# Attention probabilities turned by VectorE and DMA instead of TensorE in a fused Flamingo-style block

## The chip, the core and the metric

The kernel runs on one core of one Trainium2 chip. The core has five engines, each with its own queue of instructions that runs strictly in order: TensorE (PE, matrix products into PSUM), VectorE (DVE), ScalarE (ACT), GpSimd (POOL) and SyncE (SP, which here only issues DMA transfers). They meet through semaphores. The metric is the time of one execution on the device, in microseconds (us); less is better.

## The reference

Four steps follow each other for a batch of four sequences of 512 tokens with 512 features, all in float32:

```
x = x + tanh(g_x[0]) * ((1 - gamma) * layernorm(x) + gamma * A)          # A: sigmoid(sim), the best 30% of each row, made symmetric
x = x + tanh(g_f[0]) * bitlinear_ffn(layernorm(x))                       # Hadamard turns, 8-bit activations, ternary weights
x = x + tanh(g_x[1]) * latent_attention(layernorm(x), ctx)               # 16 heads, see below
x = x + tanh(g_f[1]) * bitlinear_glu(layernorm(x))
```

The change lies in the third step. For each head:

```
q_big  = rope(hidden @ Wq_h.T @ w_kc_q_h)      # 384 wide
kv_r   = rope(ctx)                             # 512 x 128 for a sequence, shared by all heads
scores = (q_big @ W_qr_h) @ (kv_r @ W_kr_h).T  # 64 wide product, 512 x 512 scores
attn   = softmax(scores)
ctx_c  = attn @ kv_r                           # 512 x 128
out   += ctx_c @ w_kc_kv_h.T @ Wo_h.T          # the two weights are multiplied once, ahead: "om", 128 x 512
```

## The kernel before, in words

A sequence is held as four token tiles of 128 tokens (one per partition) with 512 features. The work falls into a long prologue (first step of sequence 0, first feed-forward, weights), an attention phase from about 286 us to the end of the 32nd pair, and a tail (second feed-forward of the last sequence).

The attention phase is a generator, `attention`, that walks over 32 **pairs**: sequence `b` from 0 to 3 and in it `g` from 0 to 7, a pair being two heads of one sequence. For the pair at hand it goes over the four token tiles `j`, and mixes in the query work of the pair that comes next:

- `scores(j)` (lines 855 to 878) makes the 128 x 512 scores `pss` of both heads (two 64-row products that run side by side in the array), DVE finds the row maximum `nm` (L871), ACT takes the exponential `pp` (L874), DVE inverts the sum (L876) and ACT scales `pp` (L877).
- `head` (L804) and `rope` (L819 to L833) make the next pair's queries, products on PE, rotation on DVE and POOL (`ro`, `rs`).
- `turn(j)` turns the probabilities of a tile: four 128 x 128 products with the identity per head on PE (`ppt`, L885), copied from PSUM into `pT` by ACT (L886). It is called two tiles late (`turn(j - 2)`), and the last two calls come after the loop.
- after the loop `rotated` makes the next pair's `qr` (`pr`, L790 and L792, copied by ACT in L850); then `attended` multiplies all 512 turned rows by `kv` (`pc`, L893, copied to `cxo` by ACT in L898), and `added` multiplies by `om` and adds to the residual (`po`, L905, and DVE in L910).

A float32 product of 128 x 128 by 128 x 512 shows as two matmul records in the profile.

Beside the pairs runs background work in slices: while sequence `b` is in attention, the first step of `b + 1` (`adjacency`: a chain of MAX8 and MATCH_REPLACE8 on DVE, L486 and L491, which finds the threshold of the best 30%), its key projections (`keys`) and its feed-forward (`feed0`); during the last sequence the second feed-forward of the first three. A list of jobs with costs and due times sets how much background work each tile of a pair yields. The order on each engine is then fixed when the program is built, by a scheduler with priorities; the top-k chain carries a lowered priority and so fills the places that others leave on DVE.

All loads of weights (`wq`, `wc`, `wr`, `om`, `kr`) and the turns of quantized activations by DMA (L202) are issued from SP, in order. Every DMA of that queue uses one of eight completion semaphores in turn, and waits until the DMA that used it before has landed.

Of the kernel before, what the change touches and what calls it, by code (L numbers as in the profile page):

```python
# [9 lines left out]
F32 = mybir.dt.float32  # L10
# [5 lines left out]
P = 128  # L16
# [5 lines left out]
DC = 128  # L22
# [12 lines left out]
def flamingo_kernel(  # L35
# [51 lines left out]
    def front_t(name):  # L87
        if mine("front", 2):
            return two_k("front", 3, name)
        return wp.tile([P, 512], F32, tag="pp", name=name, bufs=7)  # L90

    def gate_t(name):
        if alone[0]:
# [597 lines left out]
    om_d, kr_d = {}, {}  # L691
    spilled = {}

    def ahead():

        cos_k = wp.tile([P, NT, DC], F32, tag="rs", name="cos_k", bufs=3)
        nc.gpsimd.dma_start(cos_k, cosk)
        sin_k = wp.tile([P, NT, DC], F32, tag="rs", name="sin_k", bufs=3)  # L700
        nc.gpsimd.dma_start(sin_k, sink)
        hf = DC // 2
        for b in range(B):
            cb = wp.tile([P, NT, DC], F32, tag="qh", name=f"cb_{b}")
            nc.gpsimd.dma_start(cb, cx[b * S : (b + 1) * S, :].rearrange("(j p) d -> p j d", p=P))
            t = const.tile([P, NT, DC], F32, tag=f"kv{b}", name=f"kv_{b}")
            nc.gpsimd.tensor_tensor(t, cb, cos_k, ALU.mult)
            rt = wp.tile([P, NT, DC], F32, tag="rs", name=f"rt_{b}", bufs=3)
            nc.gpsimd.tensor_tensor(rt[:, :, :hf], cb[:, :, hf:], sin_k[:, :, :hf], ALU.mult)
            nc.gpsimd.tensor_tensor(rt[:, :, hf:], cb[:, :, :hf], sin_k[:, :, hf:], ALU.mult)  # L710
            nc.gpsimd.tensor_tensor(t, t, rt, ALU.add)
            kv[b] = t
        yield
        for h in range(NH):
            wv = hp.tile([P, DC], F32, tag="wk", name=f"wv_{h}", bufs=3)
            nc.sync.dma_start(wv, wkckv[h])
            wo = wp.tile([P, D], F32, tag="rs", name=f"wo_{h}", bufs=3)
            nc.sync.dma_start(wo, woT[h])
            po = mm_ps(f"pO_{h}")
            nc.tensor.matmul(po, wv, wo, start=True, stop=True)  # L720
            om = wp.tile([P, D], F32, tag="cxo", name=f"oms_{h}", bufs=3)
            nc.scalar.copy(om, po)
            d = dram.tile([P, D], F32, tag=f"om{h}", name=f"omd_{h}")
            nc.gpsimd.dma_start(d, om)
            om_d[h] = d
            yield
        yield from keys(0)
# [25 lines left out]
    def hidden_T(b):  # L753
        mv, r = ln_stats([xs[b, j] for j in range(NT)], f"q{b}")
        t = hp.tile([P, NC, S], F32, tag="hT", name=f"hT_{b}", bufs=1)
        for j in range(NT):
            n = wp.tile([P, D], F32, tag="pp", name=f"nq_{b}_{j}", bufs=7)
            ln_tile(n, xs[b, j], j, mv, r)
            pt = tr_ps(f"phT_{b}_{j}")
            for c in range(NC):  # L760
                nc.tensor.transpose(pt[:, c, :], n[:, c * P : (c + 1) * P], ident)
            nc.scalar.copy(t[:, :, j * P : (j + 1) * P], pt)
        hT[b] = t
# [30 lines left out]
    class Pair:  # L794
# [41 lines left out]
        def rotated(self):  # L836

            wr, ros, u = self.wr, self.ros, self.u
            self.kr = wp.tile([P, S], F32, tag="kr", name=f"kr_{u}", bufs=1)
            nc.sync.dma_start(self.kr, kr_d[self.b, self.g])  # L840
            pr = mm_ps(f"pr_{u}")
            for o in range(3):
                at = 2 * o * 64
                halves(
                    pr, (wr[:, at : at + 64], wr[:, at + 64 : at + P]),
                    (ros[0, o], ros[1, o]) if o < 2 else (ros[2, 0], ros[2, 1]),
                    start=(o == 0), stop=(o == 2),
                )
            self.qr = wp.tile([P, S], F32, tag="qr", name=f"qr_{u}", bufs=1)
            nc.scalar.copy(self.qr, pr)  # L850
            self.pT = [
                wp.tile([P, NT, S], F32, tag="pT", name=f"pT_{u}_{i}") for i in range(2)
            ]

        def scores(self, j):

# [11 lines left out]
            for i in range(2):  # L868
                v = f"{self.u}_{i}_{j}"
                nm = small.tile([P, 1], F32, tag="nm", name=f"nm_{v}")  # L870
                nc.vector.tensor_reduce(nm, pss[i], AX.X, ALU.max, negate=True)  # L871
                pp = wp.tile([P, S], F32, tag="pp", name=f"pp_{v}", bufs=7)
                sm = small.tile([P, 1], F32, tag="sm", name=f"sm_{v}")
                nc.scalar.activation(pp, pss[i], AF.Exp, bias=nm, accum_out=sm)  # L874
                rs = small.tile([P, 1], F32, tag="rsm", name=f"rsm_{v}")
# [2 lines left out]
                self.pps[i, j] = pp  # L878

        def turn(self, j):  # L880
            for i in range(2):
                pt = tr_ps(f"ppt_{self.u}_{i}_{j}")
                pp = self.pps.pop((i, j))
                for l in range(NT):
                    nc.tensor.transpose(pt[:, l, :], pp[:, l * P : (l + 1) * P], ident)  # L885
                nc.scalar.copy(self.pT[i][:, :, j * P : (j + 1) * P], pt)  # L886

        def attended(self):
            self.cxo = []
            for i in range(2):  # L890
                pc = mm_ps(f"pc_{self.u}_{i}")
                for l in range(NT):
                    nc.tensor.matmul(  # L893
                        pc, kv[self.b][:, l, :], self.pT[i][:, l, :],
                        start=(l == 0), stop=(l == NT - 1),
                    )
                cxo = wp.tile([P, S], F32, tag="cxo", name=f"cxo_{self.u}_{i}", bufs=3)
                nc.scalar.copy(cxo, pc)  # L898
                self.cxo.append(cxo)

        def added(self):
            for j in range(NT):
                po = mm_ps(f"po_{self.u}_{j}")
                for i in range(2):
                    nc.tensor.matmul(  # L905
                        po, self.cxo[i][:, j * P : (j + 1) * P], self.oms[i],
                        start=(i == 0), stop=(i == 1),
                    )
                t = xs[self.b, j]
                nc.vector.scalar_tensor_tensor(t, po, tgx1, t, ALU.mult, ALU.add)  # L910
# [6 lines left out]
    def attention(first):  # L917


        order = [(b, g) for b in range(B) for g in range(NG)]  # L920
        cur = first
        for at, (b, g) in enumerate(order):
            nxt = begin(*order[at + 1]) if at + 1 < len(order) else None
            cur.oms = out_weights(b, g)
            fresh = nxt is not None and nxt.b != b
            for j in range(NT):
                cur.scores(j)
                if nxt:
# [8 lines left out]
                        nxt.rope(1)  # L937
                    else:
                        nxt.rope(2)
                if j > 1:  # L940
                    cur.turn(j - 2)
                yield b, g
            cur.turn(NT - 2)
            cur.turn(NT - 1)
            if nxt:
                nxt.rotated()
            cur.attended()
            cur.added()
            if g == NG - 1 and b < B - 1:
                for j in range(NT):  # L950
                    d = dram.tile([P, D], F32, tag=f"xd{b}_{j}", name=f"xd_{b}_{j}")
                    nc.sync.dma_start(d, xs[b, j])
                    spilled[b, j] = d
            cur = nxt

# [45 lines left out]
    def before(b):  # L1003
        k = keys(b)
        for n, cost in enumerate(adjacency(b)):
            yield cost
            if n % 6 == 5:

                with tc.high_priority(offset=-FILL // 4):
                    step(k, 1)  # L1010
# [168 lines left out]
```

## Time and profile before

| | |
|---|---|
| time, median of 3 runs | 2046.22 us (2045.72 to 2049.57) |
| profiled execution, span from first to last instruction | 2048.8 us |
| busy: PE, DVE, ACT, POOL | 1819.6, 1630.3, 1081.8, 336.1 us |
| mean granted TensorE clock | 0.960 |
| DMA moved | 151.90 MB, mean 74 GB/s |

The span of the profiled execution lies 2.6 us above the median of the runs, and inside their spread; nothing else of that execution's time is recorded. Busy times are sums over the span, so they are averages of stages that differ: the table of windows in the prediction shows the stages one by one. The page's groups name an instruction by line, engine and what it writes and reads, then its count, its busy time, the mean duration of one, and the idle time of the engine in front of it with what ended it. Records of instructions that follow each other on DVE overlap by some 0.06 to 0.09 us, so a mean is longer than the time that one more instruction adds.

### The profile page before, as it was taken

What the parts mean: (1) busy time and instruction counts of PE and PEld (TensorE: products, weight loads), DVE (VectorE), ACT (ScalarE), POOL (GpSimd) and SP (SyncE); (2) the same over time, 40 slices, a digit from 0 to 9 for tenths busy, and PEclk for the clock granted to TensorE, in tenths of its full rate; (3) what the DMA queues carried; (4) which work ended last, traced back from release to release, by engine and by line L of the source; (5) the groups of instructions that cost most, each with busy time, mean ns of one, the idle gap of its engine ahead of it and who ended that gap; (6) DMA issues with size and microseconds to landing.
All of it is one profiled execution on the core that took longest, in us unless ns stands there. A gap on an engine that the chain in (4) does not pass through costs nothing. (4 is left out here: it accounts for less than half of the span.)

```text
span 2048.8 us, 22947 instructions
## 1 busy us (share of the span) xinstructions
PE 1819.6 (89%) x7874; PEld 889.2 (43%) x7874; DVE 1630.3 (80%) x3305; ACT 1081.8 (53%) x1833; POOL 336.1 (16%) x316
## 2 busy tenths in 40 slices
PE   1268799999999999999999999999989999999898
PEld 0035534436554344455444444555443444444333
DVE  7989699987776999977778999778758556866785
ACT  6935454354434455453444564534786565555544
POOL 3020031123011122130111221301111210111000
PEclk6579899999999999999999999999999999999999
DMA  7451021111111222111122121111783112222011
GB/s 269 155 179 38 1 74 45 55 49 28 42 43 48 89 71 72 38 38 37 41 55 84 57 84 47 35 35 38 241 302 128 50 40 74 68 53 67 21 34 39
DMA packets 115556, 151.90 MB, mean 74 GB/s; under 512 B 57456, under 2 KB 68080, under 8 KB 112368
## 3 DMA queue, kind: packets, MB, share of 16 engines
q1 hardware_dynamic: 109968, 134.51, 22.0%
q0 software_dynamic: 4320, 14.16, 1.9%
q10 hardware_dynamic: 1152, 1.77, 0.2%
q8 instruction: 62, 1.02, 0.2%
q14 instruction: 54, 0.44, 0.1%
HBM read 117.90 MB, written 19.92 MB: 67 GB/s over the span
## 5 line engine op out<-in xcount | busy, mean ns | idle before, releaser
L833 POOL TENSOR_TENSOR ro<-ro,rs 128x512 f32<-128x512 f32 x192 | 255.4, 1333 | 1153.3 <-DVE rs L829 648.3
L874 ACT ACTIVATE pp<-pss,nm 128x512 f32<-128x512 f32 x256 | 174.6, 685 | 272.3 <-DVE nm L871 271.5
L804 PE MATMUL pqh<-hT,wq 128*128 128x512 f32 x512 | 239.7, 606 | 6.8 <-ACT pp L874 5.6
L893 PE MATMUL pc<-pT,kv 128*128 128x512 f32 x512 | 236.0, 600 | 2.7 <-ACT pT L886 2.6
L905 PE MATMUL po<-om,cxo 128*128 128x512 f32 x512 | 229.9, 597 | 0.0
L819 PE MATMUL pb<-qh,wc 128*128 128x512 f32 x384 | 189.4, 613 | 13.6 <-ACT qh L809 7.7
L486 DVE MAX8 m<-work 128x8 f32<-128x512 f32 x304 | 198.7, 684 | 0.6
L871 DVE TENSOR_REDUCE nm<-pss 128x1 f32<-128x512 f32 x256 | 167.8, 683 | 38.1 <-PE pss L866 37.9
L491 DVE MATCH_REPLACE8 work<-m,work 128x512 f32<-128x512 f32 x288 | 193.6, 678 | 0.1
L877 ACT ACTIVATE pp<-pp,rsm 128x512 f32<-128x512 f32 x256 | 178.6, 720 | 27.4 <-DVE rsm L876 26.2
L886 ACT COPY pT<-ppt 128x512 f32<-128x512 f32 x256 | 142.1, 588 | 38.5 <-PE ppt L885 38.0
L885 PEld LDWEIGHTS ppt<-ident,pp 128*128 128x128 f32 x1024 | 117.7, 142 | 96.6 <-issue 37.1
L885 PE MATMUL ppt<-ident,pp 128*128 128x128 f32 x1024 | 147.8, 279 | 10.1 <-ACT pp L877 4.4
L910 DVE SCALAR_TENSOR_TENSOR x<-po,gt,x 128x512 f32<-128x512 f32 x128 | 94.8, 745 | 68.4 <-PE po L905 67.6
L804 PEld LDWEIGHTS pqh<-hT,wq 128*128 128x128 f32 x512 | 93.1, 191 | 128.4 <-issue 89.6
L863 PE MATMUL pss<-kr,qr 64*128 64x512 f32 x256 | 143.4, 641 | 4.4 <-ACT pp L874 2.6
L905 PEld LDWEIGHTS po<-om,cxo 128*128 128x128 f32 x512 | 93.9, 190 | 119.5 <-issue 101.2
L866 PE MATMUL pss<-kr,qr 64*128 64x512 f32 x256 | 143.4, 641 | 0.7 <-DVE ro L827 0.5
L827 DVE TENSOR_TENSOR ro<-pb,cos_q 128x512 f32<-128x512 f32 x192 | 130.9, 682 | 10.3 <-PE pb L819 9.5
L893 PEld LDWEIGHTS pc<-pT,kv 128*128 128x128 f32 x512 | 91.9, 190 | 105.0 <-issue 90.4
L819 PEld LDWEIGHTS pb<-qh,wc 128*128 128x128 f32 x384 | 65.6, 189 | 113.6 <-issue 40.9
L898 ACT COPY cxo<-pc 128x512 f32<-128x512 f32 x64 | 37.4, 584 | 145.1 <-PE pc L893 144.8
(279 smaller groups left out, 3062.0 us busy)
## 6 DMA issues: line engine op xcount, KB each, us to landing
wq<-in_wqh SPq DMA_DIRECT2D x64, 256.0 KB, 2.7
om<-omd SPq DMA_DIRECT2D x64, 256.0 KB, 2.8
wc<-in_wkcq SPq DMA_DIRECT2D x32, 384.0 KB, 3.1
krd<-krs POOLq DMA_DIRECT2D x32, 256.0 KB, 2.5
kr<-krd SPq DMA_DIRECT2D x32, 256.0 KB, 2.7
sa_w1v<-in_gvT SPq DMA_DIRECT2D x8, 1024.0 KB, 5.3
sb_w1v<-in_gvT SPq DMA_DIRECT2D x8, 1024.0 KB, 5.2
wr<-in_wqr SPq DMA_DIRECT2D x32, 192.0 KB, 2.4
```

The lines of the kernel that those rows point to most:

```text
L486: nc.vector.max(m8[j], cur[j])
L491: nc.vector.match_replace(works[j], m8[j], cur[j], GONE)
L804: nc.tensor.matmul(pq, self.wqs[i][:, c, :], hT[self.b][:, c, :], start=(c == 0), stop=(c == NC - 1),)
L819: nc.tensor.matmul(pb, self.wc[:, at : at + P], self.qhs[i if i < 2 else o], start=True, stop=True)
L833: nc.gpsimd.tensor_tensor(ro, ro, rs, ALU.add)
L863: nc.tensor.matmul(*args, start=True, stop=True)
L871: nc.vector.tensor_reduce(nm, pss[i], AX.X, ALU.max, negate=True)
L874: nc.scalar.activation(pp, pss[i], AF.Exp, bias=nm, accum_out=sm)
L877: nc.scalar.activation(pp, pp, AF.Copy, scale=rs)
L885: nc.tensor.transpose(pt[:, l, :], pp[:, l * P : (l + 1) * P], ident)
L893: nc.tensor.matmul(pc, kv[self.b][:, l, :], self.pT[i][:, l, :], start=(l == 0), stop=(l == NT - 1),)
L905: nc.tensor.matmul(po, self.cxo[i][:, j * P : (j + 1) * P], self.oms[i], start=(i == 0), stop=(i == 1),)
```

## The change

`turn(j)` no longer uses PE and ACT. DVE turns each 32 x 32 block of a head's 128 x 512 probabilities in one instruction per head and tile (two heads, four tiles: eight per pair) into a tile `blocks`, which holds two token tiles of both heads and has one buffer. After every second tile, 16 DMAs from the SP queue move the blocks to the partitions where they belong (32 partitions, 64 KB each), into a `pT` that holds two token tiles `q` of both heads rather than four tiles of one head. `attended` and `added` then work per `q`: one product `pc` over both heads' columns, one ACT copy that puts the columns back in order, and the output of two token tiles. `q = 0` is done at the end of the pair; `q = 1` in the next pair, after its first tile of scores. `turn` is called in the tile's own step, not two later.

To make room, `pp` goes from 7 to 5 buffers, and only two sequences' `kv` are held; those of sequences 2 and 3 are written to DRAM and loaded again when sequence 0 or 1 has ended. The key projections of the next sequence start later in the background work.

```diff
-            self.pT = [
-                wp.tile([P, NT, S], F32, tag="pT", name=f"pT_{u}_{i}") for i in range(2)
-            ]
+            self.pT, self.cxo = {}, {}
...
         def turn(self, j):
+            q, k = divmod(j, 2)
+            if k == 0:
+                self.blocks = wp.tile([P, 16, P], F32, tag="blk", name=f"blk_{self.u}_{q}", bufs=1)
             for i in range(2):
-                pt = tr_ps(f"ppt_{self.u}_{i}_{j}")
-                pp = self.pps.pop((i, j))
-                for l in range(NT):
-                    nc.tensor.transpose(pt[:, l, :], pp[:, l * P : (l + 1) * P], ident)
-                nc.scalar.copy(self.pT[i][:, :, j * P : (j + 1) * P], pt)
+                at = (2 * i + k) * 32
+                nc.vector.transpose(
+                    self.blocks[:, :, at : at + 32],
+                    self.pps.pop((i, j)).rearrange("p (c s) -> p c s", s=32),
+                )
+            if k == 0:
+                return
+            t = wp.tile([P, NT, 4, P], F32, tag="pT", name=f"pT_{self.u}_{q}")
+            blocks = self.blocks.rearrange("p (l a) s -> p l a s", a=4)
+            for to in range(4):
+                for fro in range(4):
+                    nc.sync.dma_start(
+                        t[32 * to : 32 * to + 32, :, fro, :],
+                        blocks[32 * fro : 32 * fro + 32, :, to, :],
+                    )
+            self.pT[q] = t
...
+        def attended(self, q):
+            pc = mm_ps(f"pc_{self.u}_{q}")
+            pT = self.pT.pop(q).rearrange("p l a s -> p l (a s)")
+            for l in range(NT):
+                nc.tensor.matmul(
+                    pc, kv[self.b][:, l, :], pT[:, l, :], start=(l == 0), stop=(l == NT - 1)
+                )
+            cxo = wp.tile([P, S], F32, tag="cxo", name=f"cxo_{self.u}_{q}", bufs=3)
+            nc.scalar.copy(
+                cxo.rearrange("p (m a s) -> p a m s", m=4, a=4),
+                pc.rearrange("p (a m s) -> p a m s", m=4, a=4),
+            )
+            self.cxo[q] = cxo
...
+        def ended(p):
+            p.attended(1)
+            p.added(1)
+            if p.g < NG - 1:
+                return
...
+            if b + 2 < B:
+                kv[b + 2] = kv_tile(b + 2)
+                nc.sync.dma_start(kv[b + 2], kv_d[b + 2])
...
-                if j > 1:
-                    cur.turn(j - 2)
+                cur.turn(j)
+                if j == 0:
+                    if prev:
+                        ended(prev)
+                    cur.oms = out_weights(b, g)
+                if j == 3:
+                    cur.attended(0)
+                    cur.added(0)
                 yield b, g
-            cur.turn(NT - 2)
-            cur.turn(NT - 1)
             if nxt:
                 nxt.rotated()
-            cur.attended()
-            cur.added()
...
-            if n % 6 == 5:
+            if n % 6 == 5 and n > 28:
```

## The prediction

> **What bounds the kernel now.** The page's busy shares (PE 89%, DVE 80%) mix stages, so I read the table of windows first, cut where the pairs' `qr` copies stand (286 us the first, then every eighth pair or where the top-k chain ends):
>
> ```profile
> core 0: us, PE busy (x) PEld busy (x) DVE busy (x) ACT busy (x) POOL busy (x), PEclk, DMA share, GB/s
> 285.00:435.00 150.00, 142.17 (x450) 59.50 (x446) 147.29 (x328) 75.72 (x153) 32.11 (x27) 1.00 0.18 54
> 435.00:688.00 253.00, 237.51 (x1309) 130.28 (x1307) 191.06 (x340) 115.33 (x215) 42.82 (x40) 0.99 0.16 40
> 688.00:858.00 170.00, 161.95 (x506) 69.64 (x504) 167.31 (x377) 86.29 (x169) 34.82 (x32) 1.00 0.24 73
> 858.00:1102.00 244.00, 230.86 (x1298) 126.08 (x1296) 184.84 (x329) 113.97 (x213) 46.01 (x40) 1.00 0.16 42
> 1102.00:1273.00 171.00, 162.77 (x509) 70.01 (x508) 167.69 (x377) 86.50 (x170) 34.84 (x32) 1.00 0.23 73
> 1273.00:1524.00 251.00, 231.81 (x1288) 129.00 (x1287) 188.79 (x323) 143.06 (x235) 47.01 (x40) 0.97 0.37 119
> 1524.00:1892.00 368.00, 353.00 (x1254) 153.40 (x1252) 241.89 (x472) 213.31 (x351) 54.53 (x42) 1.00 0.27 76
> ```
>
> Three kinds of stretch. **A** (rows 1, 3, 5; 491 us, four pairs each, the top-k chain beside them): DVE is busy 482.3 us, 98%, and PE 466.9, 95%; DVE is full. **B** (rows 2, 4, 6; 748 us, four pairs each, the feed-forward beside them): PE 700.2, 94%; DVE 564.7, 75%. **C** (row 7; 368 us, seven pairs): PE 353, 96%; DVE 66%. ACT is below 60% everywhere. So what is added to DVE costs in A, what is taken from PE pays in B and C. Next the groups that the change touches and their nearest neighbours:
>
> ```profile
> L885 PE MATMUL ppt<-ident,pp 128*128 128x128 f32 x1024 | 147.8, 279 | 10.1 <-ACT pp L877 4.4 <-ACT pT L886 4.1 <-ACT hT L762 1.5
> L886 ACT COPY pT<-ppt 128x512 f32<-128x512 f32 x256 | 142.1, 588 | 38.5 <-PE ppt L885 38.0
> L491 DVE MATCH_REPLACE8 work<-m,work 128x512 f32<-128x512 f32 x288 | 193.6, 678 | 0.1
> L184 DVE TENSOR_SCALAR nq<-x,mv_q,r_q 128x512 f32<-128x512 f32 x16 | 7.9, 537 | 0.0
> L588 DVE TENSOR_TENSOR yb_f<-ya_f 128x1024 f32<-128x1024 f32 x64 | 77.8, 1222 | 5.8 <-PE pzh_f L603 4.8 <-PE ph_f L595 1.0
> ```
>
> The turns hold PE for 147.8 us (4.6 a pair). A DVE instruction over 128 x 512 float32 takes about 0.68 us. Then the DMA issues' row of a small load (count, size, us to landing), two lines of who waited for whom on the weight-load side of PE from 285 to 1892 us (us in total, times, longest), and a timeline of DVE (start, us):
>
> ```profile
> wk<-in_wkr SPq DMA_DIRECT2D x32, 64.0 KB, 1.8
> ```
>
> ```profile
> PEld pb L819 <- ACT qh L809: 36.5, 37, 2.1
> ...
> PEld po L905 <- ACT cxo L898: 16.4, 26, 0.7
> ```
>
> ```profile
> 744.62 0.68 DVE L491 MATCH_REPLACE8 work<-m,work 128x512 f32<-128x512 f32 x1
> 745.21 0.08 DVE L491 MATCH_VALUE_LOAD work<-m,work 128x8 f32 x1
> ```
>
> The successor of a 0.68 us record starts 0.59 us after it: records overlap, and one more such instruction adds about 0.60 us. A product that must wait for an ACT copy of the product just before it loses 36.5/37 = 0.99 us (`pb` after `qh`); `po` after `cxo` loses 16.4/26 = 0.63, since its first half needs only the older copy.
>
> **DVE in A.** Eight transposes a pair. The trace has none; the nearest rows of that size are 0.54 us (TENSOR_SCALAR) and 0.68 (MATCH_REPLACE8, also SBUF to SBUF), and the far bound is 1.22 for double the width, as if each element went twice. I take 0.68, adding 0.60: 4.8 us a pair, 154 us in all. In A's twelve pairs 57.6 us land on an engine with 8.7 us idle in 491: **+58 us**. What PE sheds there (55 us) pays nothing, since DVE is late.
>
> A rule speaks against the choice. The Trainium skill, "VectorE: DVE Perf Modes", section "The three transpose paths", gives 311 ns on VectorE for 128 x 128 in bf16 and 390 on TensorE, and says that VectorE turns only 32 x 32 blocks. Four such at 311 ns would be an estimated 1.24 us per instruction, and the sum below would then be near the third rival's. Here PE spends 147.8/1024 = 144 ns of busy time on one, which is why moving it away frees so little.
>
> **PE in B and C.** 19 pairs times 4.6 us, 88 us, would be the most. It isn't got in full, because DVE gets 4.8 us in the same pairs: B's DVE work goes from 565 to 622 us and PE's from 700 to 645, so they take turns in being the later one. I counted the changed kernel's instructions pair by pair in the order in which they are built, times the busy time of one of their group, and summed the larger engine of each pair: B goes from 689 to 649, C from 358 to 338. **-60 us.** (The same count for A gives +57.)
>
> **New waits on PE.** Before, `pr`, then `pc` and `po`, stand ahead of the next scores, so the copies `qr` and `cxo` are mostly hidden. In the built order of the changed kernel `pr` is followed directly by the next `pss` (`qr` between them) in 15 of B's and C's pairs, and `pc` by its own `po` in 10 (q = 0) and 11 (q = 1). 36 round trips at 0.99 us, less 17 at 0.63 that were there: **+25 us**. In the other pairs feed-forward products stand between and hide them.
>
> **The DMAs.** 1,024 of 64 KB. SP issues DMAs at starts 0.42 us apart at best (1456.96 and 1457.38), 0.52 in the run of three at 1471.33; 16 are 6.7 to 8.3 us, and the last lands 1.8 later: 9 us from the transposes to `pT`. The eighth before has landed by then (8 x 0.42 = 3.4 against 1.8), so the eight semaphores don't hold them. In packets: 64 MB in 512 B pieces, against 151.9 MB at a DMA share of 0.13 to 0.37 in these windows: room enough. For q = 1 the way is long: behind `pss` of tile 3 stand `pb` 2, `pc` 3.5, `po` 3.6, `pr` 3.1, `pss` 2.1 and `pqh` 3.7 us, 18 in all, against about 5 for the softmax, 1.2 for the transposes and 9 for the DMAs: hidden. The single `blocks` buffer costs DVE nothing for the same reason, as the next pair's first transposes come later still; within a pair, tile 2's are put just ahead of tile 3's. For q = 0 it is short. In the pair from 1619 to 1659 us tile 1's scores start at 1623.98 and its probabilities are done at 1628.5; transposes until 1629.8, `pT` at 1638.8. Without the removed turns PE would be through the last `pb` at about 1636.3: 2.5 us late. I charge that to the 10 pairs that have nothing between: **+25 us**. That pair shows the whole trade: 4.6 us shed, 2.5 and three times about 1 us waited.
>
> The SP queue behind them: `kr`, `wq`, `wc`, `wr`, `om` start up to 8 us later, and are loaded most of a pair ahead of use; without that cover it would be 3 us a pair (`wc` lands in 3.1).
>
> **The rest.** ACT loses 142 us and was not late; the copy `cxo` in another column order I leave at its 0.58. The spilled `kv` are four DMAs of 256 KB, stored beside the prologue and loaded a pair ahead of the key projections that read them. Five `pp` suffice, since they come free two tiles sooner. The key projections only move inside stretch A. At the end the last q = 1 waits for its DMAs with little beside it: 9 + 1 us against the 7 us of `pc` and `po` done by then: **+3**.
>
> **Sum:** 58 - 60 + 25 + 25 + 3 = +51 us on the profiled 2048.8, and 2.6 less for the runs' median: 2097. I state 2094, as some of the 36 round trips will fall where DVE is later anyway.
>
> **Rivals.**
> *PE's time returns (faster).* B and C are PE-bound by 94 to 96%, and 88 us shed is more than A's 58. If the waits on PE in B and C stay under (88 - 58 - 3)/19 = 1.4 us a pair, the kernel is faster; with none and all of the 88, 2046 - 27 = 2019; with a DVE transpose at the 0.54 row besides (0.14 less, 96 times in A), 2006. For it: ACT gets quicker with 142 us less, and feed-forward products fill gaps. Against it: the built order with its 36 bare places. 0.24.
> *DMAs land late (slower still).* If 16 in flight side by side land in 5 us, as 256 KB loads of `x` do (5.2), instead of 1.8, the eight semaphores make it two rounds, about 13.6 us: 4.6 more for 20 pairs, 2190. Against it: the 64 KB row. 0.12.
> *The transpose takes 1.22 us.* 4.9 us more a pair: A +59, about 30 in B where DVE becomes the later engine: 2183. 0.12.
>
> The granted clock fell to 0.97 in the one row of B with PE at 92%. PE will be 75% busy in A. The Trainium skill, "TensorE: Matmul & The Clock Gate", Part 1, states half clock after an idle window of about 3.4 us. Gaps here should stay at 1 to 3 us; a lower clock in A has PE's 137 idle us to use up before it costs.
>
> **Numbers.** My own case has 0.50 and by itself 2055 to 2135 (waits of 0.5 to 5 us a pair). To leave no more than 2 in 10 out, the range reaches most of the way into the rivals: 2018 to 2165. 0.2% (4 us) is what a measurement of this kernel can tell; faster 0.25, from the first rival and a little of mine; same 0.05; slower 0.70.
>
> **What would show it.** In the profile after: 256 transposes at 0.65 to 0.70 us on DVE; PE busy near 1675, DVE near 1785; A's stretches near 20 us longer each, with DVE at 98% and PE near 75%; B and C nearly unchanged, with `po` waiting for `cxo`, `pss` for `qr`, `pc` for the DMAs of `pT`. Wrong would be: A no longer (the transposes found room), B and C shorter by 80 (no waits), or PE waiting over 5 us a pair for `pT`.

## The result, and the profile after

| | before | after |
|---|---|---|
| time, median of the runs | 2047.89 us (4 runs, 2045.72 to 2053.69) | 2228.54 us (4 runs, 2222.91 to 2233.8) |
| ratio, 95% interval | | 1.0873 [1.0836, 1.091] |
| profiled span | 2048.8 us | 2232.0 us |
| mean granted clock of TensorE | 0.960 | 0.911 |
| busy: PE, DVE, ACT | 1819.6, 1630.3, 1081.8 us | 1790.1, 1786.9, 970.0 us |

Slower, as forecast, but by 181 us instead of about 50: 2228.5 lies above the range's end of 2165. Three readings of the kernel after answer to those of before. First the table of windows, cut again at the pairs' `qr` copies (pairs 0 to 3 and 4 to 7 of each sequence; in the last sequence pairs 0 to 6 together, then the end):

```profile
core 0: us, PE busy (x) PEld busy (x) DVE busy (x) ACT busy (x) POOL busy (x), PEclk, DMA share, GB/s
287.00:479.00 192.00, 157.52 (x378) 59.38 (x378) 183.26 (x398) 68.23 (x134) 39.90 (x38) 0.91 0.32 91
479.00:745.00 266.00, 223.69 (x1140) 113.59 (x1140) 212.10 (x380) 99.08 (x180) 38.87 (x34) 0.94 0.27 70
745.00:948.00 203.00, 170.91 (x454) 67.61 (x452) 188.38 (x418) 79.68 (x150) 45.83 (x48) 0.93 0.37 104
948.00:1210.00 262.00, 217.63 (x1092) 108.56 (x1092) 205.72 (x355) 93.45 (x173) 30.45 (x24) 0.93 0.28 71
1210.00:1412.00 202.00, 170.64 (x452) 67.59 (x452) 186.93 (x416) 79.13 (x149) 45.83 (x48) 0.93 0.37 104
1412.00:1690.00 278.00, 220.06 (x1088) 110.03 (x1086) 188.99 (x297) 125.53 (x197) 31.48 (x24) 0.91 0.45 135
1690.00:2068.00 378.00, 337.23 (x1018) 133.25 (x1018) 273.21 (x527) 187.03 (x295) 55.66 (x42) 0.96 0.41 112
2068.00:2232.00 164.00, 131.93 (x560) 57.67 (x560) 112.00 (x245) 70.64 (x110) 0.00 (x0) 0.90 0.20 52
```

With the trace of before cut at the same pairs, A (rows 1, 3 and 5) grew from 490 to 597 us, B (rows 2, 4 and 6) from 748 to 806, the rest from 524 to 542. No row shows a full engine any more: in A DVE is at 93 to 95% instead of 98, in B PE is at 79 to 84% instead of 94. Both engines wait, and in the first seven rows the clock column has fallen from between 0.97 and 1.00 to between 0.91 and 0.96. So something else ends last. The group of `pc` on the page of before, then the groups that the change touches and the row of the moves in the kernel after:

```profile
L893 PE MATMUL pc<-pT,kv 128*128 128x512 f32 x512 | 236.0, 600 | 2.7 <-ACT pT L886 2.6
```

```profile
L918 PE MATMUL pc<-pT,kv 128*128 128x512 f32 x512 | 276.6, 682 | 85.2 <-DMA pT<-blk 67.5
...
L934 PE MATMUL po<-om,cxo 128*128 128x512 f32 x512 | 244.8, 618 | 35.7 <-ACT cxo L922 34.9
...
L898 DVE STREAM_TRANSPOSE blk<-pp 128x512 f32<-128x512 f32 x256 | 166.1, 687 | 31.8 <-DMA pT<-blk 23.2
...
pT<-blk SPq DMA_DIRECT2D x1024, 64.0 KB, 2.1
```

The transpose takes 687 ns, the value that was chosen, and a move lands in 2.1 us. But `pc` waits 67.5 us for the moves, DVE itself waits 23.2 us for the blocks buffer, and one `pc` record takes 682 ns in the mean where the same 512 took 600 before. The list of waits (us in total, times, longest):

```profile
PE pc L918 <- DMA pT<-blk: 67.5, 16, 6.9
...
PE pd_f L436 <- DMA zT_f<-q_f: 49.6, 12, 11.8
...
PE po L934 <- ACT cxo L922: 34.9, 36, 6.3
PE pss L874 <- ACT qr L863: 14.6, 21, 0.7
```

Before, `pd_f` waited 6.5 us and `pss` for `qr` 0.7. Now the timelines of SP's queue and of PE, about a pair where the probabilities are late (start, us):

```profile
1758.34 10.54 SPq L908 DMA_DIRECT2D pT<-blk  x16
...
1777.69 10.25 SPq L908 DMA_DIRECT2D pT<-blk  x16
```

```profile
1742.97 3.60 PE L918 MATMUL pc<-pT,kv 128*128 128x512 f32 x8
1747.24 3.70 PE L934 MATMUL po<-om,cxo 128*128 128x512 f32 x8 [0.68 <-ACT cxo L922]
...
1770.67 5.91 PE L918 MATMUL pc<-pT,kv 128*128 128x512 f32 x8 [5.33 <-DMA pT<-blk]
...
1779.92 6.39 PE L934 MATMUL po<-om,cxo 128*128 128x512 f32 x8
```

Sixteen moves hold SP for 10.3 to 10.5 us, 0.65 us each, and `pc` starts 12.3 us after the first of them. Over all 64 halves of pairs the way, from the start of the first issue to the last landing, has a median of 11.8 us. The same eight `pc` records that took 3.60 us take 5.91, and eight `po` 6.39 instead of 3.70: after the wait PE runs at half clock.

The wait of `pd_f` comes from the same queue in part. DVE's last instruction on `q_f`, SP's queue and the product that reads the turned `zT_f`:

```profile
1135.44 1.22 DVE L215 TENSOR_SCALAR q_f<-yb_f 128x2048 bf16<-128x2048 f32 x1
```

```profile
1134.26 10.25 SPq L908 DMA_DIRECT2D pT<-blk  x16
1144.61 2.01 SPq L202 DMA_TRANSPOSE zT_f<-q_f  x1
```

```profile
1149.06 3.17 PE L436 MATMUL pd_f<-wd_w,zT_f 128*128 128x512 fp8e4 x7 [11.78 <-DMA zT_f<-q_f]
```

`q_f` is ready at 1136.66, and its turn by DMA is issued 8 us later, when the moves have left the queue. Of the twelve such turns five are held 7 to 8 us, 41 us in all twelve; in the kernel before none is held.
From 287 us on, 21 of PE's gaps are longer than 3.4 us (123.2 us together; before, none), and between the first and the last `qr` copy the granted clock is one half for 232 us in all (before: 20.5). PE's busy time stands 115 us above the 1675 that was forecast; the 212 us more at half clock can explain at most half their length, 106 us, and less where PE was idle in them.

### The profile page after: what moved, and what is told of

Read it like the earlier page. It is cut to its first block, busy times and chain, and to the rows that moved or that the text cites. A ratio compares the mean times of both kernels' runs of the same rounds, so it can differ in the third digit from the quotient of the medians.

```text
span 2232.0 us, 22311 instructions
## 1 busy us (share of the span) xinstructions
PE 1790.1 (80%) x6850; PEld 803.4 (36%) x6850; DVE 1786.9 (80%) x3561; ACT 970.0 (43%) x1587; POOL 330.8 (15%) x318
## 5 line engine op out<-in xcount | busy, mean ns | idle before, releaser
L846 POOL TENSOR_TENSOR ro<-ro,rs 128x512 f32<-128x512 f32 x192 | 249.4, 1301 | 1371.8 <-DVE rsm L887 654.6
L918 PE MATMUL pc<-pT,kv 128*128 128x512 f32 x512 | 276.6, 682 | 85.2 <-DMA pT<-blk 67.5
L934 PE MATMUL po<-om,cxo 128*128 128x512 f32 x512 | 244.8, 618 | 35.7 <-ACT cxo L922 34.9
L817 PE MATMUL pqh<-hT,wq 128*128 128x512 f32 x512 | 247.7, 624 | 16.6 <-ACT pp L885 12.2
L832 PE MATMUL pb<-qh,wc 128*128 128x512 f32 x384 | 199.6, 637 | 24.7 <-DVE ro L840 12.9
L898 DVE STREAM_TRANSPOSE blk<-pp 128x512 f32<-128x512 f32 x256 | 166.1, 687 | 31.8 <-DMA pT<-blk 23.2
L918 PEld LDWEIGHTS pc<-pT,kv 128*128 128x128 f32 x512 | 108.1, 220 | 222.4 <-issue 203.1
L874 PE MATMUL pss<-kr,qr 64*128 64x512 f32 x256 | 144.4, 645 | 23.2 <-ACT qr L863 14.6
L436 PE MATMUL pd_f<-wd_w,zT_f 128*128 128x512 fp8e4 x256 | 73.7, 454 | 49.6 <-DMA zT_f<-q_f 49.6
L335 PEld LDWEIGHTS <-wa_w 128*128 128x128 fp8e4 x1536 | 90.0, 98 | 41.0 <-issue 38.8
```

The lines of the kernel that those rows point to most:

```text
L817: nc.tensor.matmul(pq, self.wqs[i][:, c, :], hT[self.b][:, c, :], start=(c == 0), stop=(c == NC - 1),)
L832: nc.tensor.matmul(pb, self.wc[:, at : at + P], self.qhs[i if i < 2 else o], start=True, stop=True)
L846: nc.gpsimd.tensor_tensor(ro, ro, rs, ALU.add)
L874: nc.tensor.matmul(*args, start=True, stop=True)
L898: nc.vector.transpose(self.blocks[:, :, at : at + 32], self.pps.pop((i, j)).rearrange("p (c s) -> p c s", s=32),)
L918: nc.tensor.matmul(pc, kv[self.b][:, l, :], pT[:, l, :], start=(l == 0), stop=(l == NT - 1))
```

## The experiments

The theory after the result: the way from a tile pair's probabilities to `pT` is too long, since 16 DMAs of 32 partitions are issued one after the other; PE waits for it and loses its clock in the waits. The rivals: rows and sizes of the DMAs; SP's queue being held (what stands behind it is late); DVE's transposes; the new order of products by itself. All runs are given as ratios to the kernel before on the same chip.

One caution holds for all: the scheduler places the background work afresh in each variant. The chain of top-k steps falls into four pairs of a sequence in the kernel after, five in the one before and six without moves (e3), so an experiment changes more than its edit. Differences of 10 to 20 us are not read as the edit's. The last column of the table is taken from the same stretch, 287 to 2068 us, of each profiled execution; in the faster runs it takes in some of the tail, and in e12 it ends before the pairs do (618 us between that run's own first and last `qr` copy).

| run | median, us | ratio [95%] | PE at half clock, us |
|---|---|---|---|
| after | 2228.54 | 1.0873 [1.0836, 1.091] | 232 |
| e8 neither transposes nor moves | 2023.87 | 0.9864 [0.985, 0.9879] | 90 |
| e5 PE turns, new order | 2105.67 | 1.0271 [1.025, 1.0293] | 63 |
| e3 transposes, no moves | 2112.89 | 1.031 [1.029, 1.0329] | 160 |
| e4 moves, no transposes | 2154.64 | 1.0508 [1.0488, 1.0529] | 188 |
| e1 long rows | 2227.84 | 1.0871 [1.0853, 1.0888] | |
| e12 twice the moves | 2620.92 | 1.2784 [1.2756, 1.2812] | 537 |
| e9 through DRAM | 2269.52 | 1.1077 [1.105, 1.1104] | |
| e14 moves on POOL | 2251.86 | 1.0984 [1.0967, 1.1] | 251 |
| e13 `zT` on ACT | 2229.27 | 1.0873 [1.0852, 1.0895] | 223 |
| e2 SP and ACT | 2167.21 | 1.0573 [1.0553, 1.0593] | 212 |
| e16 SP and POOL | 2147.2 | 1.0458 [1.0429, 1.0487] | 197 |
| e17 SP, POOL and ACT | 2189.86 | 1.0678 [1.0646, 1.071] | 220 |
| e6 first half later | 2215.65 | 1.0794 [1.0768, 1.082] | |
| e10 both halves in the next pair | 2213.4 | 1.0795 [1.0772, 1.0818] | 252 |
| e11 the same, SP and ACT | 2375.77 | 1.1577 [1.1545, 1.1609] | |
| e7 filler | 2218.32 | 1.0811 [1.0795, 1.0827] | 149 |
| e15 filler, SP and ACT | 2150.76 | 1.0497 [1.048, 1.0515] | 113 |

**The four corners: transposes and moves, each with and without.**

e8: ACT writes the scaled probabilities straight into the blocks, and `pc` reads the blocks.

```diff
-                nc.scalar.activation(pp, pp, AF.Copy, scale=rs)
+                nc.scalar.activation(self.blocks[:, :, at : at + 32], pp..., AF.Copy, scale=rs)
-            (two nc.vector.transpose, sixteen nc.sync.dma_start)
+            self.pT[q] = self.blocks.rearrange("p (l a) s -> p l a s", a=4)
```

> Leaves out both DVE's transposes and the moves: ACT's scaling writes the unturned probabilities into the tile that the product reads, so the output is not the reference's. What is left is the new order with PE's and ACT's turns gone. Additive: without the moves 115 us go and without the transposes 74, so 2228 - 189 = 2040. Order theory: no less than 2060. If the two costs overlap (both spoil the same waits): 2045 to 2075; if PE's freed 148 us come through once nothing is in the way: 1950 to 2010.

e3 keeps the transposes and lets `pc` read the blocks; e4 keeps the moves and lets ACT write the blocks as in e8.

> Leaves out the moves: the products read the turned blocks where DVE wrote them, so the output is not the reference's. DVE's transposes, the products and their order stay; the blocks take pT's two buffers. Queue theory: most of the 180 us go, 2060 to 2110 us (the prediction's own sum without a wait for the DMAs, 2070, or a little more). DVE theory: 2170 to 2230, as DVE's work is the same. Order theory: 2150 to 2220.

> Leaves out DVE's transposes: ACT's scaling writes the probabilities straight into the blocks, unturned, so the output is not the reference's. The moves and the products stay. DVE theory: the 154 us of DVE work and with it nearly all of the loss go, 2050 to 2090 us. Queue theory: what DVE cost in the top-k stretches goes, 50 to 90 us, and the rest stays: 2140 to 2180. Order theory: above 2180.

```profile
PE 1730.2 (86%) x6850; PEld 783.9 (39%) x6850; DVE 1627.7 (80%) x3305; ACT 954.0 (47%) x1573; POOL 330.9 (16%) x318
```

This is the line of busy times of e8. With turning free PE is busy 89 us less than before, and the time falls by 1.36%, 28 us, to 16 us below the additive guess of 2040. e4 lies where the queue theory put it, e3 3 us above that theory's range and 37 below the others'. The transposes cost 91 us without moves (e3 less e8, 0.0446 of 2049) and 75 beside them (after less e4). The moves cost 132 us without transposes (e4 less e8) and 115 beside them (after less e3).

The placement of the background work differs between these runs, so here is the one stretch in which the top-k chain never runs: C, from the `qr` copy of the last sequence's first pair to that of its last (seven pairs). It takes 368.2 us before, 372.4 in e5 (below), 348.2 in e8, 353.8 in e3, 372.4 in e4 and 378.1 in the kernel after. The moves cost 24 us there, with the transposes and without, and the transposes 6, with the moves and without.

e3 also bears on the wait of `pd_f`. From its list of waits:

```profile
PE pd_f L436 <- DMA zT_f<-q_f: 58.1, 10, 15.2
```

Without a single move in SP's queue, `pd_f` waits as long for the feed-forward's turns as in the kernel after (49.6), and every turn is issued within 0.1 us of the moment when `q_f` is written: here the wait is for `q_f`, which DVE makes and which comes late. With the moves and without DVE's transposes (e4) it waits 22.5, and the turns are held in the queue for 27 us; with neither (e8) 9.0. So there are two causes, DVE's added work, by this reading, and the queue, and in the kernel after both act.

e5: the new order with PE's own turns and ACT's copies, as before.

```diff
-                nc.vector.transpose(self.blocks[:, :, at : at + 32], ...)
+                for l in range(NT):
+                    nc.tensor.transpose(pt[:, l, :], pp[:, l * P : (l + 1) * P], ident)
+                nc.scalar.copy(self.pT[q][:, :, (2 * i + k) * P : (2 * i + k + 1) * P], pt)
```

> The order alone: the products by two token tiles, half of them in the next pair, as changed; but the turns are made by PE and copied by ACT as before the change (each in its own tile's step). No blocks, no moves. Order theory (products right behind the copies they need, PE waits and clock): well above the kernel before, 2100 to 2180 us. Queue theory and DVE theory: the order costs only its bare round trips, 2050 to 2085.

The order (one product per two tiles, followed by its own `po`; half of it in the next pair) costs 2.7%, 55 us, with the work of before on every engine, as the order theory had it. That is with the rest of the change that e5 keeps: turns in their own tile's step, five buffers of `pp`, two sequences' `kv`, the later key projections. Taking the turns off PE (and the copies off ACT) then brings 83 us, if nobody else has to do them (e5 to e8).

**What makes a move slow.** e1 gives each partition one run of 2 KB (ACT's exponential writes its columns in another order) in place of four of 512 B. e12 splits each move in two of 32 KB.

```diff
-  t[32 * to : 32 * to + 32, :, fro, :],  blocks[32 * fro : 32 * fro + 32, :, to, :]
+  t[32 * to : 32 * to + 32, fro, :, :],  blocks[32 * fro : 32 * fro + 32, to, :, :]      # e1
+  t[..., l : l + 2, fro, :],  blocks[..., l : l + 2, to, :]   for l in (0, 2)           # e12
```

> The block moves carry one run of 2 KB per partition (32 rows per DMA) instead of four runs of 512 B (128 rows); ACT's exponential writes its columns in that order, and the product reads four strided runs. Bytes and the number of DMAs stay. Queue theory: SP needs 0.60 us to issue one move (0.33 for most other loads), 16 take 10 us, the products wait for the last, loads and turns behind them are late, and PE's clock halves in the waits; if the rows set the issue time, it falls towards 0.33, 16 take 5.5 to 7 us, and the kernel comes to 2110 to 2170 us. If the issue time stays at 0.60 the queue theory expects no change. DVE theory (the added transposes on a full DVE are the loss) and order theory (products right behind the copies they need are the loss): 2210 to 2245 in any case.

> Each move is cut in two (same bytes, 64 DMAs a pair, 2,048 in all). Queue theory: SP is held 20 us per half pair, which no product hides, so the price per move of the changed kernel repeats or grows: 2228 plus 150 to 400 us. If moves cost by bytes or by landing: 2228 to 2270.

e1 changes nothing: 588 ns for an issue, against 599. In e12 half as large a move still takes 595 ns, and 1,024 more of them bring 392 us:

```profile
L919 PE MATMUL pc<-pT,kv 128*128 128x512 f32 x512 | 330.7, 798 | 385.3 <-DMA pT<-blk 381.2
...
L898 DVE STREAM_TRANSPOSE blk<-pp 128x512 f32<-128x512 f32 x256 | 165.2, 687 | 279.7 <-DMA pT<-blk 257.5
```

Bytes and rows are the same or fewer, the number of DMAs decides. The way has a median of 22.0 us in e12, 11.5 in e1.

e9 stores the blocks to DRAM in one DMA of 128 partitions and loads `pT` in four of 32.

```diff
+            nc.sync.dma_start(d, self.blocks)
-                for fro in range(4): nc.sync.dma_start(t[32 * to ...], blocks[32 * fro ...])
+                nc.sync.dma_start(t[32 * to : 32 * to + 32], d.rearrange(...)[to])
```

> The moves go through DRAM: one store of all blocks (128 partitions, 1 MB) and four loads of 32 partitions, 256 KB each, so SP issues 5 DMAs per half pair instead of 16; the way is one store and one load long, 4 to 6 us plus 3, after the transposes, about what 16 issues and a landing take (12). Queue theory, in its form that SP's occupancy delays all else (loads, DMA turns of the feed-forward): 2120 to 2170. In its form that only the way to pT counts: 2190 to 2240, no gain. Beside it: if a load of 32 partitions issues in 0.60 us too, the number of partitions sets the issue time; if in 0.33 to 0.43, that both ends lie in SBUF.

The two tiles' queue lines (ns min/median/max of one issue):

```profile
L908 SPq DMA_DIRECT2D pT<-bd x256: 558/628/1277, 305.6 to 2148.5; - x128
...
L906 SPq DMA_DIRECT2D bd<-blk x64: 319/325/532, 300.7 to 2142.7; - x64
```

An issue of 128 partitions takes 325 ns, one of 32 takes 628, from DRAM as from SBUF. SP's issuing falls from 614 us to 182 (64 x 0.325 + 256 x 0.628), and the kernel is yet slower by 41 us: the store lands after 4.6 us and the loads after 5.4, one behind the other. The way has a median of 12.9 us, and `pc` waits 74.7 us for it. Both ranges of the expectation were missed on the slow side, the second, in which only the way counts, by 30 us. So freeing SP for 430 us gains nothing where the way stays long.

**Whose queue.** e14 puts all moves on POOL, e13 leaves them and puts the feed-forward's `zT` turns (L202) on ACT.

```diff
-                    nc.sync.dma_start(            # L908
+                    nc.gpsimd.dma_start(          # e14
-            nc.sync.dma_start_transpose(dst, src)     # L202
+            nc.scalar.dma_start_transpose(dst, src)   # e13
```

> The one edit against the changed kernel: all 1,024 moves are issued by POOL instead of SP. POOL is busy 331 us, so its time is not scarce. Theory A (SP's time is what costs: all that stands behind the moves on SP is late): the waits of pd_f for zT and of the loads go, and the time falls below that of two queues, 2,167. Theory B (the way from the transposes to pT costs, whoever issues): if POOL takes as long or longer per move, the waits of pc for pT stay at 60 us or more and, as POOL's additions for the rotation stand behind the moves, the waits of pr for them appear; 2,220 or more.

> The one edit against the changed kernel: the feed-forward's turns zT by DMA (line 202) are issued by ACT instead of SP; the 1,024 moves stay on SP. Theory (the feed-forward's turns stand in SP's queue behind 16 moves of 0.6 us, which is why pd_f waits 49.6 us instead of 6.5): pd_f's wait falls to 10 us or less and 25 to 40 us of the time come back, about 2,190 us. Rival (the wait for zT is for its data, or hides other waits): pd_f's wait stays over 30 us, or falls and the waits for pT grow by as much; within 10 us of 2,228.

The page's group of the moves in e14, and the waits of e13:

```profile
L908 POOL DMA_DIRECT2D pT<-blk x1024 | 569.1, 564 | 180.1 <-issue 65.0
```

```profile
PE pc L918 <- DMA pT<-blk: 54.2, 17, 5.7
...
PE pd_f L436 <- DMA zT_f<-q_f: 24.2, 9, 4.5
```

POOL takes 0.56 us for one, so the way is as long (median 11.8), `pc` waits 62.9 us for it, and the time is 23 us longer although SP's queue is free of moves. The waits of `pr` that its theory B added didn't come (4.3 us). Together with e9 this says that SP being held is not what costs most. e13 halves the wait for `zT` (49.6 to 24.2; no turn is held over 0.5 us any more) and gains nothing. Its time is the rival's, though none of the rival's signs came: the wait fell below 30 us, and that for `pT` fell too. Nor does e13 show that the hold is free, since ACT, which has the copies, now issues the turns: C takes 400.6 us with it, against 378.1.

e2 deals the moves to SP and ACT, e16 to SP and POOL, e17 to all three.

```diff
-                    nc.sync.dma_start(
+                    (nc.scalar if fro % 2 else nc.sync).dma_start(                            # e2
+                    (nc.gpsimd if fro % 2 else nc.sync).dma_start(                            # e16
+                    (nc.sync, nc.gpsimd, nc.scalar)[(4 * to + fro) % 3].dma_start(            # e17
```

> Half of the 16 moves are issued from ACT's queue, the other half from SP's. Queue theory: the last move is issued after 5 us instead of 10, so pT comes 4 to 5 us sooner: 2120 to 2175 us, with ACT's queue holding about 10 us more a pair (ACT was busy 43%). DVE theory and order theory: 2210 to 2245; if ACT's issues delay its own copies, more than 2245.

> The one edit against the changed kernel: every second move is issued by POOL, the others by SP. The way to pT is then as short as with SP and ACT (8 moves of about 0.6 us on each queue), but ACT, which has the softmax and the copies cxo and qr to do, issues none. Theory (only the length of the way counts, whoever's queue it is): as with SP and ACT, 2,167, within 15 us. Rival (half of what two queues could give was lost on ACT, where the exponentials and copies stand behind 8 issues of 5 us): 2,130 or less.

> The changed kernel with the 16 moves of a half dealt in turn to SP, POOL and ACT: 5 or 6 on each queue, 3.0 to 3.6 us of issuing in place of 10.2. Theory (the way counts, and what it costs falls with it): below two queues, 2,130 to 2,155, with no wait of pc for pT over 1 us. Rival (two queues have already hidden the way behind the other work, and what is left is the order's and the clock's): 2,160 to 2,175.

The issuing is about halved, and the way falls from 11.8 us to 8.1 (e2) and 8.0 (e16), medians again. That brings 61 us with ACT, within the queue theory's range, and 81 with POOL. No wait of `pc` for `pT` is listed any more. In e16, though, `pc` is listed with 24 us of waits for DMAs whose data it doesn't read:

```profile
PE pc L918 <- DMA kr<-krd: 10.1, 6, 2.6
...
PE pc L918 <- DMA wq<-in_wqh: 7.6, 4, 3.0
...
PE pc L918 <- DMA wc<-in_wkcq: 4.8, 2, 2.8
```

These loads follow the moves on SP and share its eight semaphores, and all of the 14 waits that make up the 24 us end 0.2 to 0.9 us after the last move of their half has landed. So they are waits for the moves, which e16 still has; e2 has none. What ACT loses by issuing is in the waits of e2; e16 has no such line:

```profile
ACT pp L885 <- DMA pT<-blk: 110.0, 19, 11.1
ACT qr L863 <- DMA pT<-blk: 103.2, 14, 10.1
```

ACT's exponentials and copies stand in its queue behind moves that wait their turn. With three queues ACT is in again (81.0 us on `qr`), a move lands after 3.6 to 4.3 us instead of 3.0 to 3.3, and 43 us are lost against e16: neither side of its expectation held, nor of e16's, which came out between the two. The third queue doesn't shorten the way: its median is 8.0 us, as with two, since what the issuing saves the landing takes back. So e17 doesn't test a shorter way. That ACT's part is the reason for the 43 us is read from these waits; no run isolates it from the placement. In e16 the way is 8 x 0.60 + 3.2 = 8 us, near the 9 us of the forecast, and it lies 34 us above e3, which has no moves at all and, like e16, the top-k chain in six pairs.

**Moving the consumer instead.** e6 puts the first half's `pc` and `po` behind `rotated`; e10 puts both halves in the next pair (after tile 0 and tile 1); e11 is e10 with SP and ACT.

```diff
-                if j == 3:
-                    cur.attended(0)
-                    cur.added(0)
+            cur.attended(0); cur.added(0)          # e6, after nxt.rotated()
+                if j == 0 and prev: half(prev, 0)  # e10, e11
+                if j == 1: ended(prev)
```

> The changed kernel, with the product and output of q = 0 after the next pair's qr products instead of ahead of them: its blocks have 3 us more to land, and qr's copy is hidden behind pc and po. Queue theory: of 67 us that pc waits for the moves some 40 go, with the clock that falls in them 20 more: 2150 to 2195. Order theory: the 15 us of pss behind qr and more go: 2150 to 2200. DVE theory: 2215 to 2240.

> The changed kernel, with both halves of the product in the next pair (q = 0 after its first tile's scores, q = 1 after its second's), so that every move has at least 18 us of products ahead of its reader; the same 32 moves on SP. If the wait for the moves is what costs (67 us of PE idle, and the clock that falls in it): 2110 to 2160. If SP's occupancy by 20 us of issues a pair is: 2190 to 2230.

> The two together: both halves of the product in the next pair, and every second move issued from ACT's queue. If occupancy and wait are separate costs: 2080 to 2130. If two queues had only shortened the wait: no better than both halves in the next pair alone.

In e10 the wait for `pT` is gone from PE, and another has come:

```profile
PE pr L803 <- POOL ro L846: 94.4, 26, 8.5
```

The timelines of PE, DVE and POOL around one such wait (start, us):

```profile
1788.76 0.64 PE L803 MATMUL pr<-ro,wr 128*64 128x512 f32 x1 [4.56 <-POOL ro L846]
```

```profile
1781.78 1.29 DVE L898 STREAM_TRANSPOSE blk<-pp 128x512 f32<-128x512 f32 x2
...
1785.90 1.39 DVE L845 TENSOR_TENSOR rs<-pb,sin_q 64x512 f32<-64x512 f32 x2
```

```profile
1787.43 1.27 POOL L846 TENSOR_TENSOR ro<-ro,rs 128x512 f32<-128x512 f32 x1 [0.86 <-DVE rs L845]
```

No product of the pair stands any more between the last `rope` and `pr`, so PE sees the whole chain, rotation on DVE until 1787.3 and addition on POOL until 1788.7, and transposes stand ahead of it in DVE's queue. Of the 67.5 us, 15 come back. The time lies in the range of the occupancy theory (2190 to 2230) and not of the wait theory, but the waits show another reason, and e9 and e14 speak against occupancy. e6 is the same on a smaller scale (`pc` 22.7, `pr` 54.7), a miss for the queue and the order theory, with 13 us won; that its time is at the edge of the DVE theory's range (2215 to 2240) is by the caution above no support for it. e11 missed both its ranges: 147 us slower, PE waiting 77.1 us for `qr` and 62.6 for `cxo`, ACT's copies. Taking away the named wait isn't taking away its cause.

**The clock.** e7 gives PE 32 turns of the identity per pair that nothing uses; e15 the same with SP and ACT.

```diff
+            if q == 0:
+                for r in range(8):
+                    pt = tr_ps(f"fill_{self.u}_{r}")
+                    for l in range(NT):
+                        nc.tensor.transpose(pt[:, l, :], ident, ident)
```

> The changed kernel, with 32 turns of the identity per pair on PE ahead of the product of q = 0, that nobody reads: PE's work is back at its old amount (148 us more). Clock theory: PE stood at half clock for 232 us of the attention phase, which costs about half of it; if the filler falls into the waits and keeps the clock up, the time goes down, 2150 to 2215. If the clock doesn't matter, or the fill falls beside the waits: 2228 to 2330.

> The changed kernel with every second move issued by ACT and with 32 turns of the identity by TensorE in each pair (about 148 us more work for TensorE, its results used by nothing). Theory (with waits shorter, TensorE's clock is what is left; filler keeps it up): about 2,150 to 2,165, with less time below the full clock than the 212 us of two queues alone. Rival (with shorter waits TensorE's own work decides again): slower than two queues alone, 2,190 or more.

As much work as the change took from PE is given back to it, and the kernel is no slower: 10 us faster (e7, 3 us outside the clock theory's range), or 16 against e2 (e15, within it), which by the caution above are not read as gains. Half clock falls from 232 to 149 us, and from 212 to 113. So PE's freed 148 us were worth nothing in these two kernels. That the higher clock pays for the added work is a reading; the filler also fills the wait (`pc` waits 27.9 us for `pT` instead of 67.5), and no run separates the two.

No variant that computes the reference is faster than the kernel before; e5, closest to it, is 2.7% slower.

## Why the prediction was wrong in size

- **The transpose's price** held: 687 ns against 0.68, DVE busy 1786.9 against "near 1785". Its cost came out in sum: 58 us in A and 28 in B and C, where it cut PE's 88 to 60, are 86; measured 91 (e3 less e8). Where it falls did not: from e8 to e3 A loses 23 us, B gains 109 and C 6, as the top-k chain moved from five pairs to six. So the agreement is partly luck.
- **PE's relief**, 88 us for B and C, is close to the 83 measured from e5 to e8, but by luck: of these, 40 lie in A, where the forecast had it pay nothing, 17 in B and 24 in C (seven pairs, 32 forecast). In the kernel after it cannot be seen: PE's busy time fell by 29.5 us instead of some 145, as the records got longer, and e7 shows that giving the work back costs nothing there. The forecast summed busy times at full clock.
- **New waits on PE, +25**: right as waits, about 30 too small as the price of the order, which e5 puts at 55 us. In e5 `po` waits 18.3 us for `cxo` (26 times) and `pss` 8.9 for `qr` (13 times), 27 us; in the kernel after it is `po` 36 times 0.97 us and `pss` 21 times 0.70. Half clock stands 38 us longer in e5 than before (58.3 against 20.5 between the first and the last `qr` copy), which is worth 19 us at most. What makes up the rest stays open; A alone is 53 us longer, B and C together 9, and the placement of the background work, with the chain in four pairs instead of five, may be part of it.
- **The DMAs, +25: the step that failed.** The forecast took 0.42 to 0.52 us per issue from loads of 128 partitions. An issue of 32 partitions takes 0.60 (e1, e9, e12: whatever its rows, source or size), 16 take 10.3 instead of 6.7 to 8.3, and the way is 12 us instead of 9. So `pT` came late 16 times, by 4.2 us in the mean and 6.9 at most, instead of 10 times by 2.5. Measured: 115 to 132 us for the moves, of which `pc`'s waits are 67.5; the clock, DVE's wait for the blocks and the held turns `zT` have a share that no run divides. Where e16 makes the way 8 us the moves cost 34, so the rest of that step's reasoning was about right for the way it assumed.
- **"Gaps here should stay at 1 to 3 us"** and so leave the clock alone: wrong twice. Those of `pc` reached 6.9 us, and shorter ones cost clock as well (below). The Trainium skill, "TensorE: Matmul & The Clock Gate", Part 1, has half clock after an idle window of about 3.4 us and full clock after a busy one. The window's length agrees with this trace; that it must be idle does not, as 6 of 10 windows with PE 40 to 50% busy were followed by half clock.
- **"The single `blocks` buffer costs DVE nothing"**: it cost 23.2 us of waits, six of them, up to 6.7 us, as the moves read the buffer until the next transposes want it.
- **SP's queue behind the moves** was called harmless. For the loads it was: no product that reads `kr`, `wq`, `wc`, `wr` or `om` has a listed wait for them. The prediction overlooked that the turns `zT` stand in the same queue: they are held up to 8 us, and the three longest gaps of PE in the attention phase (10.1 to 11.8 us) end with them. What that costs in time no run isolates.
- **The rivals.** DMAs landing late (2190) came nearest, with the wrong mechanism: landing stayed at 2.1 us (1.8 was assumed), issuing was slow. The transpose at 1.22 us fell, and PE's time did not return in the kernel after; it shows where both the moves and the transposes are left out (e8).

From the kernel before to the one after by way of the runs, then: order +55 (e5), PE's relief -83 (e8), transposes +91 (e3), moves +115, together +178 of the 181 measured. The steps were forecast at +28 (the end's 3 with them), -88, +86 and +25. On the other way round, by e4, the moves are 132 and the transposes 75, so the terms are good to some 15 us. In C, where the chain is not in the way, the four are +4, -24, +6 and +24.

## What to carry to other kernels

Work taken from an engine that is 94% busy is worth only what the new path doesn't take back: before moving it, lay the whole way from producer to consumer end to end (instructions times issue time, then the landing), with issue times from rows of the same partition count and with what else stands in the same queue, and compare it with the work that stands between. A named wait that is moved out of the way shows the next chain behind it, so the check is the time, not the wait. And a TensorE that waits a few microseconds per step can pay a second time in clock: here its half-clock time rose from 20.5 to 232 us.

## What the runs showed of the hardware

**The clock is decided on a fixed grid of 3.41 us.** In the kernel after, all half-clock stretches in the attention phase start at the same phase of a 3.41 us grid, and last one to four such windows. I cut PE's records by that grid. At full clock, a window with PE busy under 40% was followed by half clock in 31 of 31 cases, 40 to 50% in 6 of 10, over 50% in 3 of 414. At half clock, a window under 80% was never followed by full clock (0 of 26), one over 80% always (40 of 40). The other 18 traces, cut in the same way between the first and the last `qr` copy, agree in the main, with exceptions at 80%: under 40% 437 of 437, 40 to 50% 73 of 161, over 50% 38 of 7,594; back to full clock under 80% 3 of 459, over 80% 560 of 619. So a few waits that add up to some 2 us in one window can suffice: at 812.6 us the longest gap of the window before was 1.0, and 21 of the 40 stretches had no gap over 3.4 us before them.

**An issue of 32 partitions takes longer than one of 128 on SP and ACT**: 325 ns for 128 on SP (e9's store) and 334 on ACT (`cos_q` in the kernel after, one issue), about 600 for 32 on SP (599) and ACT (615). On POOL there is next to none: 549 for 32 (e14), and 542 for the 128 of `krd` (the kernel after). What in the issue makes the difference no run shows.

**Landing grows with queues side by side**: 2.1 us on SP alone, 2.3 on POOL alone, 2.5 to 2.6 on SP and ACT, 3.0 to 3.3 on SP and POOL, 3.6 to 4.3 on three.
